# Fusing tokenizer and transformer on one core: the last weighted sum is handed over two images later, and the projection's loads get six buffers

## The chip, the cores and the metric

The kernel runs on one core of a Trainium2 chip, alone. The metric is device time in microseconds for one launch, and the number compared is the median of several executions. One execution is also recorded by the hardware profiler; that one has its own time and its own span (first to last instruction on the core).

Engine names in what follows: PE is the matrix engine (TensorE), DVE is VectorE, ACT is ScalarE, POOL is GpSimd, SP is SyncE. The first four compute; in the part of the kernel that matters here SP issues the large loads, and POOL issues the gathers, the scatters and the output.

## The reference, cut to what matters

A tokenizer of four Fourier layers (truncated 2-D FFT, per-mode mixing, pointwise mixing, batch norm) turns 64 images of 256 x 256 into 256 rows of width 256 each. 77 text rows are added to each, which gives 333 tokens. Then one pre-norm transformer layer follows, in which half of the tokens go through the feed-forward net:

```python
h = tok(x)                                  # 64 x 256 x 256, last step out = v @ q_w + q_b
h = concatenate([h, txt], axis=1)           # 64 x 333 x 256
h = h + attn(layernorm(h))                  # one head of width 256
z = layernorm(h)
weights = z @ wr + br                       # one router weight for each token
_, idx = top_k(weights, 166); sel = idx[:, :165]
y = (gelu(z[sel] @ w1 + b1) @ w2 + b2) * weights[sel]
h = h + (zeros.at[sel].set(y) + z)
```

The last line is the one concerned: for each token, the feed-forward row if it was selected (a zero row if not) times its router weight, plus the normalised row z and the residual h.

## The kernel before

The tokenizer's layers take the first 9.6 ms and are written in an order fixed by hand. The change touches only what follows. There the code is written as plain functions, image by image, and a scheduler orders the instructions of each engine: it weighs up, with costs of its own, what could start when. So the place of a call in the source is a wish, and the order in which an engine meets its instructions is that of the built program. [...]

For one image b these functions are called:

- `image_rows` projects the last Fourier layer to 256 rows. Eight chunks `ch` of 1 MB each are loaded from HBM by SP (line 909) and reduced by 32 matmuls (line 911, four for each chunk) into the accumulator `hp`, which ACT copies out as `h` (line 916). Chunks come from the pool `inp`; before the change it has seven buffers. SP can issue a load only once the matmuls that read the old content of the buffer are done.
- `attention`: layer norm (lines 922 to 943, the square root by ACT in line 928), queries (1009, 1013), scores (1023), softmax (1028 to 1030), values (1037, 1040), transposed probabilities (1052), product (1061), the sum with `h` and a bias added by POOL (1057, 1064). The second layer norm gives `fz`, stored by POOL in a table in HBM (line 1069).
- `select` ranks the tokens: it computes the router weights (955 to 962) and then, for three groups of tokens, the rank and a 0/1 matrix `place` (970 to 982), all on DVE.
- `fetch` turns `place` into row numbers `who` with small matmuls (994, two sets of three, and 997) and gathers the 165 selected rows as `zr` by two indirect DMAs from POOL (998).
- `feed_forward` transposes `zr` (1079, copied out as `zs`), multiplies by w1 (1087, eight blocks; ACT copies each out as `g` with the gelu, line 1091), multiplies by w2 (1098, 1102), transposes back (1108), stores the rows `ys` in a second table in HBM (POOL, 1111), gathers them back to token order as `o` by three indirect DMAs from POOL (1115; tokens that were not selected fetch a zero row), and adds `z` to the residual on POOL (1118).
- `finish` is the last weighted sum: three instructions on DVE (line 1124), `o * fw + h1`, then 17 stores to the output from POOL (1129, 1133).

All POOL transfers carry one of eight semaphores in turn, and a transfer waits until the one eight before it has landed. PSUM accumulators named `pp` come from a pool of six, so a block of line 1087 can start when the accumulator six places before it has been copied out.

The loop at the end of the program is a software pipeline. In turn b it calls the rows of image b+2, the attention of b+1 (with the fetch of b inside it), the finish of b-1, the feed-forward of b, and the selection of b+1.

Of the kernel before, what the change touches and what calls it, by code (L numbers as in the profile page):

```python
# [9 lines left out]
F32 = mybir.dt.float32  # L10
# [128 lines left out]
def tile_fno_fusion_transformer(ctx: ExitStack, tc: tile.TileContext, a, cst_d, grid_d, out):  # L139
    nc = tc.nc  # L140
    x = a["x"].rearrange("b x y o -> b x (y o)")
    B = x.shape[0]
# [7 lines left out]
    def tables(pool, first, last, name):  # L150

        lo, hi = _AT[first][0], _AT[last][0] + _AT[last][1]
        t = pool.tile([128, hi - lo], F32, name=name)
        nc.sync.dma_start(t, cst_d[:, lo:hi])
        return lambda k: t[:, _AT[k][0] - lo:_AT[k][0] - lo + _AT[k][1]]
# [623 lines left out]
    src = vd[L % 2]  # L779
    s_, t_ = st  # L780
    tcon = ctx.enter_context(tc.tile_pool(name="tcon", bufs=1))
    inp = ctx.enter_context(tc.tile_pool(name="inp", bufs=7))
    tabt = tables(tcon, "exT", "tri", "cstt")
    EXT, MASK4, IOTA = tabt("exT"), tabt("mask4"), tabt("iota")
    TOKN = tabt("tokn").rearrange("p (t n) -> p t n", t=3)
# [15 lines left out]
    D = S  # L801
# [69 lines left out]
    tp = ctx.enter_context(tc.tile_pool(name="tt", bufs=2))  # L871
# [5 lines left out]
    def psum():  # L877
        return pp.tile([128, 512], F32, name="pp")
# [124 lines left out]
    def attention(b, h, between=None):  # L1003
        z, zT = layer_norm(h, "a")
        qT = tp.tile([128, 2, TOK], F32, name="qT")
        for eh in range(2):
            ps = psum()
            for dh in range(2):
                nc.tensor.matmul(
                    ps[:, :TOK], lhsT=wqk[:, dh, 128 * eh:128 * eh + 128], rhs=zT[:, dh, :],  # L1010
                    start=dh == 0, stop=dh == 1,
                )
            nc.scalar.activation(qT[:, eh, :], ps[:, :TOK], AF.Identity, bias=bqk[:, eh:eh + 1], scale=1.0)
        if between:
            between()
        v = tp.tile([128, 3, D + 2], F32, name="v")
        p_ = tp.tile([128, 3, TOK], F32, name="prob")
        sm = small.tile([128, 3], F32, name="sm")
        for t in range(3):
            r = rows[t]  # L1020
            ps = psum()
            for eh in range(2):
                nc.tensor.matmul(  # L1023
                    ps[:r, :TOK], lhsT=qT[:, eh, toks[t]], rhs=zT[:, eh, :], start=eh == 0, stop=eh == 1
                )
            scale = 1.0 / D ** 0.5
            mx = small.tile([128, 1], F32, name="mx")
            nc.vector.reduce_max(mx[:r], ps[:r, :TOK], axis=AX.X)
            nc.vector.tensor_scalar_mul(mx[:r], mx[:r], -scale)
            nc.scalar.activation(  # L1030
                p_[:r, t, :], ps[:r, :TOK], AF.Exp, bias=mx[:r], scale=scale, accum_out=sm[:r, t:t + 1]
            )
        for t in range(3):
            r = rows[t]
            ps = psum()
            for dh in range(2):
                nc.tensor.matmul(  # L1037
                    ps[:r, :D + 2], lhsT=zT[:, dh, toks[t]], rhs=wvE[:, dh, :], start=dh == 0, stop=dh == 1
                )
            nc.vector.tensor_add(v[:r, t, :], ps[:r, :D + 2], bvE[:r])  # L1040
            nc.vector.reciprocal(sm[:r, t:t + 1], sm[:r, t:t + 1])

            for n in range(2):
                nz = small.tile([128, 1], F32, name="nz")
                nc.vector.tensor_scalar(nz[:r], v[:r, t, D + n:D + n + 1], 0.0, None, ALU.not_equal)
                nc.vector.tensor_mul(sm[:r, t:t + 1], sm[:r, t:t + 1], nz[:r])
        pT = tp.tile([128, 3, TOK], F32, name="probT")
        for jt in range(3):
            r = rows[jt]
            ps = psum()  # L1050
            for t in range(3):
                nc.tensor.transpose(ps[:r, toks[t]], p_[:rows[t], t, toks[jt]], ID[:rows[t], :rows[t]])
            evict(pT[:r, jt, :], ps[:r, :TOK], 2)
        h1 = tp.tile([128, 3, D], F32, name="h1", bufs=3)
        for t in range(3):
            r = rows[t]
            nc.gpsimd.tensor_add(h[:r, t, :], h[:r, t, :], boB[:r])  # L1057
            ps = psum()
            for jt in range(3):
                rj = rows[jt]  # L1060
                nc.tensor.matmul(  # L1061
                    ps[:r, :D], lhsT=pT[:rj, jt, toks[t]], rhs=v[:rj, jt, 0:D], start=jt == 0, stop=jt == 2
                )
            nc.vector.scalar_tensor_tensor(
                h1[:r, t, :], ps[:r, :D], sm[:r, t:t + 1], h[:r, t, :], ALU.mult, ALU.add
            )
        z = layer_norm(h1, "f")
        for t in range(3):
            nc.gpsimd.dma_start(z_d[b % 3][128 * t:128 * t + rows[t]], z[:rows[t], t, :])  # L1069
        return h1, z  # L1070

    def feed_forward(b, h1, z, fw, idx, place, zr):

        zs = tp.tile([128, 2, KEPT], F32, name="zs")
        ps = psum()
        for c, k in enumerate(kept):
            n = k.stop - k.start
            for dh in range(2):
                nc.tensor.transpose(
                    ps[:, KEPT * dh + k.start:KEPT * dh + k.stop], zr[:n, c, 128 * dh:128 * dh + 128], ID[:n, :n]  # L1080
                )
        evict(zs.rearrange("p h k -> p (h k)"), ps[:, :2 * KEPT], 2)
        g = tp.tile([128, HID // 128, KEPT], F32, name="g", bufs=1)
        for hb in range(HID // 128):
            ps = psum()
            for dh in range(2):
                nc.tensor.matmul(  # L1087
                    ps[:, :KEPT], lhsT=w1[:, dh, 128 * hb:128 * hb + 128], rhs=zs[:, dh, :],
                    start=dh == 0, stop=dh == 1,
                )  # L1090
            nc.scalar.activation(
                g[:, hb, :], ps[:, :KEPT], AF.Gelu_apprx_tanh, bias=b1c[:, hb:hb + 1], scale=1.0
            )
        yT = tp.tile([128, 2, KEPT], F32, name="yT")
        for dh in range(2):
            ps = psum()
            for hb in range(HID // 128):
                nc.tensor.matmul(
                    ps[:, :KEPT], lhsT=w2[:, hb, 128 * dh:128 * dh + 128], rhs=g[:, hb, :],
                    start=hb == 0, stop=hb == HID // 128 - 1,  # L1100
                )
            nc.scalar.activation(yT[:, dh, :], ps[:, :KEPT], AF.Identity, bias=b2c[:, dh:dh + 1], scale=1.0)
        ys = tp.tile([128, 2, D], F32, name="ys")
        for c, k in enumerate(kept):
            n = k.stop - k.start
            ps = psum()
            for dh in range(2):
                nc.tensor.transpose(ps[:n, 128 * dh:128 * dh + 128], yT[:, dh, k], ID)
            evict(ys[:n, c, :], ps[:n, :D], 2)
        for c, k in enumerate(kept):  # L1110
            nc.gpsimd.dma_start(y_d[b % 3][k], ys[:k.stop - k.start, c, :])
        o = tp.tile([128, 3, D], F32, name="o")
        for t in range(3):
            r = rows[t]
            nc.gpsimd.indirect_dma_start(  # L1115
                o[:r, t, :], None, y_d[b % 3][:, :], bass.IndirectOffsetOnAxis(ap=idx[:r, t:t + 1], axis=0)
            )
            nc.gpsimd.tensor_add(h1[:r, t, :], h1[:r, t, :], z[:r, t, :])  # L1118
        return o, h1, fw

    def finish(b, o, h1, fw):
        for t in range(3):
            r = rows[t]
            nc.vector.scalar_tensor_tensor(  # L1124
                o[:r, t, :], o[:r, t, :], fw[:r, t:t + 1], h1[:r, t, :], ALU.mult, ALU.add
            )
        for g in range(4):
            for n in range(4):
                nc.gpsimd.dma_start(  # L1129
                    out[b, 64 * n + 16 * g:64 * n + 16 * g + 16].rearrange("(p t) d -> p t d", t=2),  # L1130
                    o[32 * g + 8 * n:32 * g + 8 * n + 8, 0:2, :],
                )
        nc.gpsimd.dma_start(out[b, S:TOK], o[0:TXT, 2, :])
# [1 line left out]
    hs = {n: image_rows(n) for n in range(min(2, B))}  # L1135
    done = attention(0, hs.pop(0))
    done += select(0, done[1])
    last = None
    for b in range(B):
        now, got = done, []  # L1140
        if b + 2 < B:
            hs[b + 2] = image_rows(b + 2)
        if b + 1 < B:
            done = attention(b + 1, hs.pop(b + 1), lambda: got.append(fetch(b, now[-1])))
        else:
            got.append(fetch(b, now[-1]))
        if last:
            finish(b - 1, *last)
        last = feed_forward(b, *now, *got)
        if b + 1 < B:  # L1150
            done += select(b + 1, done[1])
    finish(B - 1, *last)


# [31 lines left out]
```

## Time and profile before

| what | value |
|---|---|
| median of 3 runs | 12,647.37 us (12,644.53 to 12,658.94) |
| the profiled execution | 12,662.01 us, span 12,660.2 us |
| busy over the span | PE 88%, DVE 70%, ACT 48%, POOL 16% |
| from 9,811 to 12,541 us, the steady part of the loop | 2,730 us, PE busy 2,365.65 us, granted PE clock 0.90, DMA engines 64% |
| the fetches of line 998 in that part | one every 44.7 us on average |

The steady part is what the change touches: 64 images, of which all but the first and the last few follow one pattern of about 44.7 us. "Granted clock" is the share of full speed that the chip allows PE; the trace records it as intervals. The DMA share is the mean busy share of the core's 16 DMA engines in a stretch. In the waits view a line reads: who waited, at which line, for whom, then microseconds in total, number of times, longest.

### The profile page before, as it was taken

The numbers are of one execution on the slowest core, as the hardware profiler recorded it, in microseconds if no ns is written. First come the engines' busy times: TensorE is split into PE (matmuls) and PEld (weight loads), VectorE is DVE, ScalarE is ACT, GpSimd is POOL, SyncE is SP. The second block draws the span as 40 slices with busy tenths as digits, with TensorE's granted clock in tenths as the row PEclk, the third lists the DMA queues.
The fourth block names the chain that finished last, engine by engine and source line by source line (L and its number), as shares of the span: only waits on it lengthen the run. The fifth ranks groups of instructions, "written<-read, shape, count | busy, mean of one in ns | idle before, by whom it ended". The sixth has DMA issues, their size and how long they took to land. (4 is left out here: it accounts for less than half of the span.)

```text
span 12660.2 us, 404578 instructions
## 1 busy us (share of the span) xinstructions
PE 11148.0 (88%) x181142; PEld 5823.2 (46%) x181142; DVE 8876.0 (70%) x10892; ACT 6048.8 (48%) x10153; POOL 2037.2 (16%) x2630
## 2 busy tenths in 40 slices
PE   6999999997999999999979999999996888888887
PEld 3444444443444444444434444444443555555555
DVE  6777777777777777767667767677775666666665
ACT  5555555555555555545545545555553333333333
POOL 0000000001000000000010000000001455555555
PEclk7999999998999999999989999999997899889888
DMA  6555555556899998988888989889898666666664
GB/s 226 202 201 203 201 201 200 200 201 221 350 352 353 350 354 344 352 340 349 336 314 347 351 341 355 344 338 349 348 352 286 222 223 228 226 228 232 225 224 149
DMA packets 648775, 3550.85 MB, mean 280 GB/s; under 512 B 136632, under 2 KB 187320, under 8 KB 248056
## 3 DMA queue, kind: packets, MB, share of 16 engines
q1 hardware_dynamic: 539520, 3392.85, 69.8%
q0 software_dynamic: 100368, 128.39, 4.2%
q8 instruction: 1417, 23.22, 0.7%
q10 hardware_dynamic: 7144, 3.72, 0.1%
q14 instruction: 326, 2.67, 0.1%
HBM read 1794.51 MB, written 1729.56 MB: 278 GB/s over the span
## 5 line engine op out<-in xcount | busy, mean ns | idle before, releaser
L669 ACT ACTIVATE ring<-ring 128x1024 f32<-128x1024 f32 x3072 | 3108.8, 1012 | 1192.8 <-PE ring L662 1154.5
L650 DVE STREAM_TRANSPOSE t<-vo 128x2048 f32<-128x2048 f32 x1536 | 3549.9, 2311 | 174.9 <-ACT vo L645 14.4
L662 PE MATMUL ring<-vo,w 32*32 32x512 f32 x49152 | 2852.8, 622 | 391.2 <-DVE zt L689 138.9
L645 ACT ACTIVATE vo<-ring 128x1024 f32<-128x1024 f32 x1536 | 1568.2, 1021 | 3006.2 <-PE ring L638 2392.4
L646 DVE TENSOR_SCALAR vo<-ring 128x1024 f32<-128x1024 f32 x1536 | 1858.1, 1210 | 603.6 <-PE ring L638 415.0
L679 PE MATMUL ring<-t,cst 32*32 32x512 f32 x49152 | 1874.4, 605 | 311.4 <-issue 310.6
L689 DVE STREAM_TRANSPOSE zt<-ring 128x1024 f32<-128x1024 f32 x384 | 711.5, 1924 | 1678.5 <-PE ring L679 1678.5
L597 POOL TENSOR_TENSOR ams<-am,sk 48x512 f32<-48x512 f32 x384 | 486.9, 1268 | 8650.8 <-DMA am<-mix 8331.5
L662 PEld LDWEIGHTS ring<-vo,w 32*32 32x32 f32 x49152 | 763.6, 105 | 1905.2 <-ACT ring L669 478.6
L679 PEld LDWEIGHTS ring<-t,cst 32*32 32x32 f32 x49152 | 974.6, 104 | 1172.2 <-issue 726.6
L638 PE MATMUL ring<-vin,ws 32*32 32x512 f32 x32768 | 1239.5, 608 | 23.6 <-issue 21.6
L1129 POOL DMA_DIRECT2D out_dram<-o x1024 | 530.0, 530 | 808.4 <-DVE gt L979 394.2
L702 PEld LDWEIGHTS ring<-cst,zt 128*128 128x128 f32 x4608 | 535.4, 194 | 173.3 <-ACT vo L645 162.5
L669 ACT ACTIVATION_READ_ACCUMULATOR ring<-ring 128x1 f32 x3072 | 584.2, 190 | 0.0
L702 PE MATMUL ring<-cst,zt 128*128 128x96 f32 x4608 | 567.7, 280 | 6.7 <-DVE zt L689 6.7
L911 PE MATMUL hp<-ch,win 128*32 128x512 f32 x4096 | 469.0, 602 | 12.8 <-DMA ch<-v 12.7
L638 PEld LDWEIGHTS ring<-vin,ws 32*32 32x32 f32 x32768 | 253.4, 103 | 407.9 <-issue 375.7
L608 PE MATMUL ring<-ams,cst 49*128 49x512 f32 (+1 forms) x1536 | 391.5, 621 | 34.5 <-POOL ams L597 25.0
L1023 PE MATMUL pp<-azT,qT 128*128 128x333 f32 (+1 forms) x768 | 411.5, 690 | 0.0
L1124 DVE SCALAR_TENSOR_TENSOR o<-o,fw,h 128x256 f32<-128x256 f32 (+1 forms) x192 | 92.7, 483 | 397.7 <-DMA o<-yr,idx 262.4
L994 PE MATMUL pp<-cstt,place 128*83 128x2 f32 (+3 forms) x768 | 110.3, 248 | 282.4 <-DVE place L982 264.2
L1087 PE MATMUL pp<-zs,w 128*128 128x165 f32 x2048 | 319.6, 316 | 41.2 <-DVE zs L181 24.5
(940 smaller groups left out, 12260.0 us busy)
## 6 DMA issues: line engine op xcount, KB each, us to landing
v<-vo SPq DMA_DIRECT2D x1536, 1024.0 KB
vin<-v SPq DMA_DIRECT2D x1024, 1024.0 KB
ch<-v SPq DMA_DIRECT2D x512, 1024.0 KB
mix<-ob SPq DMA_DIRECT2D x96, 512.0 KB
am<-mix SPq DMA_DIRECT2D x384, 96.0 KB
xin<-in_x_dram SPq DMA_DIRECT2D x16, 1024.0 KB
mv<-in_x_dram SPq DMA_DIRECT2D x256, 64.0 KB
zr<-fz POOLq DMA_DIRECT2D x128, 128.0 KB, 2.0
```

The costliest lines, as they stand in the source:

```text
L597: nc.gpsimd.tensor_tensor(ams[b % 2][hv], a_[hv], sk[hv].rearrange("p c k -> p (c k)"), ALU.mult)
L638: nc.tensor.matmul(ps[n][32 * j:32 * j + 32], lhsT=ws[32 * n:32 * n + 32], rhs=v[32 * n:32 * n + 32, 2 * j:2 * j + 2, :], start=False, sto ...
L645: nc.scalar.activation(of[:, 0:2], t2[0], AF.Relu)
L646: nc.vector.tensor_scalar(of[:, 2:4], t2[1], 0.0, None, ALU.max)
L650: nc.vector.transpose(t32[b, t // 2][:, :, 8 * (t % 2):8 * (t % 2) + 8, :].rearrange("p y s c -> p s y c"), o.rearrange("p s (y l) -> p s ...
L662: nc.tensor.matmul(ps[n][32 * j:32 * j + 32], lhsT=w4[i + 1][32 * n:32 * n + 32], rhs=o[32 * n:32 * n + 32, 2 * j:2 * j + 2, :], start=Tru ...
L669: nc.scalar.activation(t2[n], t2[n], AF.Square, accum_out=acc[:, at:at + 1])
L679: nc.tensor.matmul(ps[n][32 * j:32 * j + 32], lhsT=FYT[32 * n:32 * n + 32, k, :], rhs=t32[b, j][32 * n:32 * n + 32, k].rearrange("p s c -> ...
L689: nc.vector.transpose(zt[:, h].rearrange("p k c -> p c k"), t2[h].rearrange("p n (s c) -> p c (n s)", c=C),)
L702: nc.tensor.matmul(ps[:, 0, 96 * g:96 * g + 96], lhsT=zt[:, h, k0:k0 + 4, :].rearrange("p k c -> p (k c)"), rhs=FX[:, h, 48 * r:48 * r + 9 ...
L911: nc.tensor.matmul(hp[32 * g:32 * g + 32], lhsT=win[:, 7 - t:39 - t], rhs=ch[:, g], start=False, stop=t == 7, skip_group_check=True,)
L1129: nc.gpsimd.dma_start(out[b, 64 * n + 16 * g:64 * n + 16 * g + 16].rearrange("(p t) d -> p t d", t=2), o[32 * g + 8 * n:32 * g + 8 * n + 8 ...
```

## The change

Three edits. `finish` is called for image b-2 instead of b-1, with a list that holds two pending results; to keep the data alive, `h1` has four buffers instead of three and `o` three instead of two. And the pool `inp` for the projection's chunks has six buffers instead of seven.

```diff
@@ -779,7 +779,7 @@
-    inp = ctx.enter_context(tc.tile_pool(name="inp", bufs=7))
+    inp = ctx.enter_context(tc.tile_pool(name="inp", bufs=6))
@@ -1051,7 +1051,7 @@
-        h1 = tp.tile([128, 3, D], F32, name="h1", bufs=3)
+        h1 = tp.tile([128, 3, D], F32, name="h1", bufs=4)
@@ -1109,7 +1109,7 @@
-        o = tp.tile([128, 3, D], F32, name="o")
+        o = tp.tile([128, 3, D], F32, name="o", bufs=3)
@@ -1135,7 +1135,7 @@
-    last = None
+    last = []
     for b in range(B):
         now, got = done, []
@@ -1144,12 +1144,13 @@
             done = attention(b + 1, hs.pop(b + 1), lambda: got.append(fetch(b, now[-1])))
         else:
             got.append(fetch(b, now[-1]))
-        if last:
-            finish(b - 1, *last)
-        last = feed_forward(b, *now, *got)
+        if len(last) > 1:
+            finish(b - 2, *last.pop(0))
+        last.append(feed_forward(b, *now, *got))
         if b + 1 < B:
             done += select(b + 1, done[1])
-    finish(B - 1, *last)
+    for b, q in zip(range(B - len(last), B), last):
+        finish(b, *q)
```

## The prediction

> **What bounds the kernel now.** I read the waits of a steady stretch first (10,500 to 12,400 us, 43 images), then stretches of 4 us through one image for the clock, then the instructions of single engines.
>
> ```profile
> POOL out_dram L1129 <- DVE gt L979: 303.3, 43, 8.1
> ...
> PE pp L994 <- DVE place L982: 183.0, 43, 6.8
> ...
> DVE o L1124 <- DMA o<-yr,idx: 179.1, 102, 5.4
> ...
> PEld hp L911 <- DMA ch<-v: 25.1, 30, 2.3
> ...
> PE pp L1079 <- DMA zr<-zr,who: 11.9, 15, 2.4
> ```
>
> PE waits 4.3 us in every image (183.0/43) at line 994 for the third `place`. On DVE that `place` stands behind the final sum, which waits for the gather of `o` (179.1/43 = 4.2 us). PE hardly waits for anything else: 0.3 us an image for `zr`. So gather of `o`, sum, `place`, PE is the chain.
>
> PE's own list of one image, from the first chunk matmul:
>
> ```profile
> 11156.19 7.07 PE L911 MATMUL hp<-ch,win 128*32 128x512 f32 x64
> 11163.20 2.51 PE L1009 MATMUL pp<-azT,wqk 128*128 128x333 f32 x8
> 11165.55 0.39 PE L994 MATMUL pp<-cstt,place 128*83 128x2 f32 x4
> 11171.06 0.44 PE L994 MATMUL pp<-cstt,place 77*83 77x2 f32 x2 [5.12 <-DVE place L982]
> ```
>
> And what the stall does to the clock (columns: stretch, its length, busy PE, weight load, DVE, ACT, POOL, granted clock, DMA share, GB/s):
>
> ```profile
> 11164.00:11168.00 4.00, 1.94 (x11) 1.26 (x9) 1.05 (x4) 1.91 (x3) 0.00 (x0) 1.00 0.96 281
> 11172.00:11176.00 4.00, 4.00 (x13) 2.56 (x12) 2.19 (x10) 2.00 (x3) 3.07 (x2) 0.50 1.02 412
> 11180.00:11184.00 4.00, 3.61 (x21) 2.76 (x20) 3.12 (x22) 2.82 (x9) 0.00 (x0) 1.00 0.80 260
> 11184.00:11188.00 4.00, 3.48 (x19) 2.64 (x17) 2.89 (x8) 0.52 (x1) 2.02 (x4) 1.00 0.11 27
> ```
>
> After the gap PE runs at half clock until 11,178.75 (the clock's intervals: 10.24 us at 0.5 from 11,168.5). So a gap of 5 us costs about 3.5 us more. The same lines show the DMA engines full until 11,184, with the chunk loads.
>
> There are two kinds of image in turn: in A, ACT copies out `zs`; in B, DVE does. ACT's list around line 1091 in an A:
>
> ```profile
> 11142.94 0.43 ACT L179 COPY zs<-pp 128x330 f32<-128x330 f32 x1 [4.41 <-PE pp L1079]
> 11143.40 1.28 ACT L928 ACT_TABLE_LOAD   x1
> 11144.69 0.30 ACT L928 ACTIVATE frs<-fmv,epsc 128x3 f32<-128x3 f32 x1
> 11145.00 1.28 ACT L1091 ACT_TABLE_LOAD   x1
> 11146.30 2.42 ACT L1091 ACTIVATE g<-pp,b1c 128x165 f32<-128x165 f32 x8
> ```
>
> PE meanwhile runs line 1087 from 11,143.43 for 4.76 us and goes straight on to line 1098 (11,148.03): ACT's two table loads cost PE nothing here.
>
> [...] half-clock intervals of 3.41, 6.83 or 10.24 us, after gaps of about 2 us or more. [...] Here `zr` lands 1.4 us (spread 0.5) after the last chunk packet of the burst, whereas the first gather's time from issue varies between 10.5 and 15.7 us: it is the burst that sets the landing. [...] The trace shows the 1.28 us alone; the next operation starts 0.02 us later, and I use that.
>
> **The change part by part.** The order on each engine can be read from the built program before it runs.
>
> *The final sum.* It doesn't move. In both programs DVE meets the sum of tile `o` of an image between line 974 and line 976 of the next selection, right after POOL has issued that same `o`'s gather; POOL's 17 stores follow that gather in both. The scheduler hoists the later call to the place of the earlier one. So the wait of 4.2 us stays, and with it PE's gap and half clock: 0 gained. The added buffers of `o` and `h1` take away waits that don't show: 0. Nor does the tail of the program change: POOL's list of the last four images is the same but for single swaps.
>
> *The gather of `zr`.* `who` now comes right after `place` (before, layer-norm statistics stood between), and the first gather goes ahead of the sixth store, so it's issued some 0.9 us earlier (11,172.62, with the previous store over at 11,171.76 and one store 0.53). I count 0: the burst sets the landing. If that cover is gone, at most 0.9 us in A, where PE waits for `zr`.
>
> *The sixth buffer.* PE's lists from line 911 to 1023:
>
> ```
> before, A  911x28 943 1009x2 911x4 1009x2 994x3 1023 994x3 1023x5
> after,  A  911x24 943 1009x4 911x4 994x3 1023 994x3 1023x2 911x4 1023x3
> before, B  911x32 1009x4 994x3 1023 994x3 1023x2 ...
> after,  B  911x24 1009 911x4 1009x3 994x3 1023 911x4 994x3 1023x5
> ```
>
> The seventh chunk comes later, but still ahead of the stall. Its load is issued when the first chunk is used, as the eighth's was before; that arrived in time for a use 6.2 us into the projection, but for waits of 0.8 us (25.1/30). The new use is at 5.6 us in B and later in A: up to 1.4 us more, all inside the stall. The eighth chunk goes behind the stall. That is 8 of the 64 matmuls, 7.07 x 8/64 = 0.88 us, taken from a place where PE would wait anyway and added to where it is late. [...] I take 0.88 (0 if something later hides it; 1.77 if it's all paid at half clock). In B PE reaches line 1079 1.3 us after `zr` has landed (30.74 against 29.43 us after the first chunk matmul): all 0.88 counts. In A PE waits there for `zr` on average 11.9/21 = 0.57 us: 0.31 counts. The second half of the gather comes later in B (`who` waits behind the displaced chunk), some 0.7 us, which B's 1.3 us hide. SP's list keeps its order, the loads are the same 8 MB, and DMA is 64% busy: 0.
>
> *ACT's list.* `h` now comes later, so the square root of its layer norm does too, and the table loads (!) stand elsewhere:
>
> ```
> before, A  qT h qT !ars !prob x3 probT zs !frs !g x8
> after,  A  qT qT !prob h prob x2 probT !ars zs !g !frs !g x7
> before, B  h qT !ars qT !prob x3 probT x2 !frs !g x8
> after,  B  qT qT h !prob x3 !ars probT x2 frs !g x8
> ```
>
> B has one load fewer; it stands where line 1037 covers it: 0. A has one more, and it splits `g`: between the first and the second come load, `frs`, load: 1.28 + 0.30 + 1.28 = 2.86 us. On the times shown: line 1087 starts at 43.43 and the first block's `g` load about 0.9 later, at 44.35 to 45.63; `g` until 46.05, then 2.86, second `g` done at 49.3. The eighth block of 1087 needs that accumulator (six in the pool) and would start at 43.43 + 7 x 0.595 = 47.6. PE waits 1.75 us, and behind it in PE's list the rest of the feed-forward net, the next image's transposes and its chunk matmuls. Bounds: 0, and the 2.86. Line 1098 afterwards uses a `g` each 0.29 us, as fast as ACT delivers: no more.
>
> *Moved layer-norm work on DVE* (three `az`, 1.6 us) now stands between the sums of line 1064. PE's accumulators for the fifth block are needed 2.6 us after the last of these sums was done before: 0, with 1 us left.
>
> *Sum.* The new patterns hold for 28 images A and 27 B: 28 x (0.31 + 1.75) + 27 x 0.88 = 57.7 + 23.8 = 81.5 us. The profiled execution, 12,662.0, becomes 12,743.5. It stands 14.6 above the median of the runs; so 12,729.
>
> **Rivals.**
>
> 1. *Hidden after all.* The accumulators come free in time and something else takes up the displaced chunk: 12,647. For it: PE has 0.3 to 0.5 us of small waits in the image. Against it: B's PE is late at line 1079 by its own list.
>
> 2. *The new stall halves the clock.* 1.75 us is just below the gaps of 2.0 us that did so in this trace, and 1.6 with 0.5 did. One interval of 3.41 us costs 1.7: 28 x 1.7 = 48 more, 12,777; with the upper bounds of both terms (28 x 3.74 + 27 x 1.77 = 152) up to 12,850.
>
> 3. *The sum does run on older data*, the faster side. If in truth the sum meets data that landed an image ago, PE loses its gap (4.3) and the half clock (3.5): 55 x 7.8 = 430 us, 12,220. It decides only if `zr` then lands within 22 us of the first chunk matmul, when PE would get to it (7.07 + 2.51 + 0.39, then 15.97 from 11,171.06 to line 1079 less half of the 7.69 at half clock); from 24 us on a new gap of 2 us brings the half clock back at line 1079. `zr` lands at 29 to 30 with the burst, so even then most is lost. The order of the lists speaks against it.
>
> **How the numbers follow.** The sum as worked out: 0.52, own range 12,690 to 12,770. Half clock as well: 0.20. Hidden: 0.18. Faster, rival 3 or a gain that I don't see: 0.10. Within 0.2%, 25 us, is about what a measurement of this kernel can't tell from no change. Slower by more: 0.70, the first two without a low end of 0.02; the same 0.20; faster 0.10. The range, 12,640 to 12,815, leaves out the faster case and the top of rival 2.
>
> **What would show it.** Line 1124 waits for `o` as before, about 4 us an image, and line 994 for `place` too. Four matmul rows of line 911 stand after line 994. ACT shows in every second image a `g`, two table loads and seven `g`; line 1087 there waits about 1.7 us for ACT. The step from fetch to fetch is 46 to 46.3 us instead of 44.7. I'm wrong if the wait at line 1124 is gone, if line 1087 doesn't wait, or if the granted clock in the steady part moves by more than 0.02 from 0.90.

## The result

The changed kernel takes 12,746.33 us (median of four runs, 12,723.01 to 12,756.72), the kernel before 12,652.57 us beside it. The ratio is 1.0072, with a 95% interval of 1.0054 to 1.0089: slower by 94 us. The profiled execution took 12,756.72 us, with a span of 12,754.9 us against 12,660.2. The first 9,617 us, ahead of the loop that the change touches, are as they were (PE busy 8,613.92 us there, 8,617.85 before).

The waits of the steady stretch of the changed kernel, from 10,500 to 12,400 us (who waited, at which line, for whom: us in total, times, longest). The stretch now holds 41 images instead of 43:

```profile
DVE o L1124 <- DMA o<-yr,idx: 265.7, 123, 5.2
...
PE pp L994 <- DVE place L982: 203.2, 41, 6.7
...
PE pp L1087 <- ACT g L1091: 33.8, 19, 1.8
...
PEld hp L911 <- DMA ch<-v: 24.9, 29, 2.8
...
PE pp L1079 <- DMA zr<-zr,who: 4.9, 7, 1.1
```

The chain from the gather of `o` over the sum of line 1124 to `place` is still there: PE waits 203.2/41 = 5.0 us an image for `place`. The wait for `zr` has shrunk because PE now comes later; `zr` itself lands when it did (its landing times are given further down). One line is new: line 1087 waits for ACT's `g`, 33.8/19 = 1.78 us, in every second image.

One line of the kernel before has to be set beside these. Its wait at line 1124 stands in two lines of the view, and the prediction read only the first:

```profile
DVE o L1124 <- issue: 94.8, 25, 5.5
```

Together they are (179.1 + 94.8)/43 = 6.4 us an image, against 265.7/41 = 6.5 after. The wait didn't grow; it is only credited differently.

PE's own list of one image A of the changed kernel (start, busy us, engine, line, operation, count, and in brackets the idle time before it; the trace shows each matmul of these lines as two, so x8 is one chunk):

```profile
11161.59 1.06 PE L911 MATMUL hp<-ch,win 128*32 128x512 f32 x8 [0.25 <-DMA ch<-v]
11162.59 0.46 PE L994 MATMUL pp<-cstt,place 128*83 128x2 f32 x4
11167.87 0.44 PE L994 MATMUL pp<-cstt,place 77*83 77x2 f32 x2 [4.83 <-DVE place L982]
...
11172.70 1.94 PE L911 MATMUL hp<-ch,win 128*32 128x512 f32 x8
...
11186.00 4.20 PE L1087 MATMUL pp<-zs,w 128*128 128x165 f32 x28 [0.53 <-ACT zs L179]
11191.98 0.83 PE L1087 MATMUL pp<-zs,w 128*128 128x165 f32 x4 [1.78 <-ACT g L1091]
```

The seventh chunk's eight matmuls stand ahead of the stall, the eighth's behind it, at half clock (1.94 us instead of 1.06; the trace records a clock of 0.5 from 11,166.15 to 11,176.39). The load that they wait for had landed at 11,166.68, 1.19 us before the end of the gap of 4.83 us, but they start only at 11,172.70, in their place in PE's list. Further down, the eighth block of line 1087 waits. ACT's list of the same image shows why:

```profile
11185.51 0.43 ACT L179 COPY zs<-pp 128x330 f32<-128x330 f32 x1 [2.83 <-PE pp L1079]
11186.91 1.28 ACT L1091 ACT_TABLE_LOAD   x1 [0.96 <-PE pp L1087]
11188.20 0.40 ACT L1091 ACTIVATE g<-pp,b1c 128x165 f32<-128x165 f32 x1
11188.62 1.28 ACT L928 ACT_TABLE_LOAD   x1
11189.91 0.30 ACT L928 ACTIVATE frs<-fmv,epsc 128x3 f32<-128x3 f32 x1
11190.23 1.28 ACT L1091 ACT_TABLE_LOAD   x1
11191.52 2.14 ACT L1091 ACTIVATE g<-pp,b1c 128x165 f32<-128x165 f32 x7
```

Load, one gelu, load, square root, load, seven gelus. PE's eighth block starts at 11,191.98, right after the second gelu.

The stall at line 1087 leaves the clock of this image alone: it is 1.00 in both stretches of 4 us (stretch, length, busy PE, weight load, DVE, ACT, POOL, granted clock, DMA share, GB/s):

```profile
11188.00:11192.00 4.00, 2.22 (x17) 1.97 (x15) 1.70 (x8) 3.93 (x7) 1.74 (x4) 1.00 0.00 0
11192.00:11196.00 4.00, 4.00 (x28) 4.00 (x29) 3.34 (x6) 2.06 (x7) 2.93 (x5) 1.00 0.26 85
```

Over 9,811 to 12,541 us the granted clock is 0.89, against 0.90 before.

Where the time went, taken from the start times of all images but the first six and the last nine, in the profiled execution of each kernel. T is the first chunk matmul of line 911, F the first matmul of line 1079 that follows it in the same turn of the loop. The kinds A and B of image are those of the prediction:

| us | before | after | difference |
|---|---|---|---|
| T to F, image B | 30.80 | 31.53 | +0.73 |
| T to F, image A | 30.46 | 30.97 | +0.51 |
| F of B to the next T | 13.91 | 14.02 | +0.11 |
| F of A to the next T | 14.14 | 15.85 | +1.71 |
| mean step from F to F | 44.65 | 46.15 | +1.50 |

All 63 steps together are 97.8 us longer.

### The profile page after: what moved, and what is told of

It is laid out like the page before. It is cut to its first block, busy times and chain, and to the rows that moved or that the text cites. A ratio compares the mean times of both kernels' runs of the same rounds, so it can differ in the third digit from the quotient of the medians.

```text
span 12754.9 us, 404420 instructions
## 1 busy us (share of the span) xinstructions
PE 11182.9 (88%) x181142; PEld 5786.1 (45%) x181142; DVE 8797.6 (69%) x10892; ACT 6060.9 (48%) x10151; POOL 2039.7 (16%) x2630
## 5 line engine op out<-in xcount | busy, mean ns | idle before, releaser
L669 ACT ACTIVATE ring<-ring 128x1024 f32<-128x1024 f32 x3072 | 3108.8, 1012 | 1188.5 <-PE ring L662 1151.9
L911 PE MATMUL hp<-ch,win 128*32 128x512 f32 x4096 | 536.7, 655 | 15.3 <-DMA ch<-v 14.9
```

What stands on the lines that cost most here:

```text
L669: nc.scalar.activation(t2[n], t2[n], AF.Square, accum_out=acc[:, at:at + 1])
L911: nc.tensor.matmul(hp[32 * g:32 * g + 32], lhsT=win[:, 7 - t:39 - t], rhs=ch[:, g], start=False, stop=t == 7, skip_group_check=True,)
```

## The experiments

Most of these kernels fix one place in an engine's list with an edge that sets the order of issue and makes nothing wait for an end:

```python
def behind(ins, first):          # ins is issued after first, on the same engine
    tc.add_manual_dep(ins.ins, first.ins.name, mybir.DependencyInfo(
        mybir.DependencyClass.NoSync, mybir.DependencyReason.DATA), reason="order")
```

The line numbers of these kernels are 8 to 20 higher than those of the kernel before; the text gives the original ones.

### The sixth buffer alone

```diff
-    inp = ctx.enter_context(tc.tile_pool(name="inp", bufs=7))
+    inp = ctx.enter_context(tc.tile_pool(name="inp", bufs=6))
```

> The kernel before with one edit: the pool of the chunk loads has six buffers; the call of the last sum stays one image later and no other buffer is added. Theory (all of the loss comes from the sixth buffer, through the order of instructions that it brings about): PE's and ACT's lists are those of the changed kernel, so the ratio to before is its 1.007, 12,735 to 12,755 us, with a fetch step of 46.2 us and a wait of 1.8 us for ACT at line 1087 in every second image. Rival (the later call costs too: in the changed kernel the wait for o on DVE grew from 4.2 to 6.5 us an image): 12,670 to 12,720. If the later call gains and hides a larger loss of the buffer: 12,780 or more.

Measured: 12,750.61 us, ratio 1.0083 (1.0070 to 1.0097). The step is 46.11 us, and the waits of the same stretch of this kernel show line 1087 waiting for ACT:

```profile
PE pp L1087 <- ACT g L1091: 35.6, 20, 1.8
```

PE's and ACT's lists in its trace are those of the changed kernel. So the buffer alone gives the whole loss, and the later call with its two extra buffers gives nothing that can be measured beside six buffers. The rival here leaned on a growth of the wait for `o`, which, as shown above, didn't happen. The opposite experiment, the later call with seven buffers, was not run.

### The changed kernel without the split gelus

```diff
-        nc.scalar.activation(rs, mv[:, :, 1], AF.Sqrt, ...)
+        mark[name] = nc.scalar.activation(rs, mv[:, :, 1], AF.Sqrt, ...)
...
-            nc.scalar.activation(g[:, hb, :], ..., AF.Gelu_apprx_tanh, ...)
+            gelu = nc.scalar.activation(g[:, hb, :], ..., AF.Gelu_apprx_tanh, ...)
+            behind(gelu, mark["f"])
```

> The changed kernel, with the gelus of line 1091 held behind the square root of the next image's second layer norm (line 928) in ACT's list; no other list changes. Theory: the table loads between the first and the second gelu are worth what PE waits there, 1.75 us in each of 28 images A: 49 us less than the changed kernel, 12,690 to 12,705 us; step ending in A falls from 45.0 to about 43.2, step ending in B stays 47.4 us. Rival (PE's 1.8 us at line 1087 would only move to the next wait, for place): 12,735 or more.

Measured: 12,709.24 us, ratio 1.0039 (1.0025 to 1.0053). The wait of line 1087 for ACT is gone from the waits of that stretch, and F of A to the next T falls from 15.85 to 14.27 us, while T to F stays (31.47 and 30.86). The expectation named the wrong step: A's stall comes after A's own F, so it is the step that ends in B that falls (47.4 to 45.7 us). The gain is (1.0072 - 1.0039) x 12,655 = 42 us, a little under the 49 expected and, by the intervals of the two ratios, uncertain by some 28 us; the 63 steps of the two traces differ by 49.5 us. The stall was real time and didn't move on to the next wait.

### The changed kernel with all chunk matmuls ahead of line 994 again

```diff
-                nc.tensor.matmul(hp[32 * g:32 * g + 32], ...)
+                mark["rows"] = nc.tensor.matmul(hp[32 * g:32 * g + 32], ...)
...
-                nc.tensor.matmul(ps[:n, 2 * c:2 * c + 2], lhsT=place[:r, t, k], ...)
+                m = nc.tensor.matmul(ps[:n, 2 * c:2 * c + 2], lhsT=place[:r, t, k], ...)
+                behind(m, mark["rows"])
```

> The changed kernel, with the small matmuls of line 994 held behind the last chunk matmul of line 911, which gives PE the order it had before, with six buffers and the later call kept; ACT's list goes back to that of before by itself. Theory (order costs, not the number of buffers): 12,650 to 12,665 us, step 44.7 to 45.0; the eighth load is issued 0.9 us later than before, which may add a wait of up to 0.3 us at line 911. Rival (with six buffers the chunks are late): line 911 waits over 1 us an image and the time stays at 12,700 or more.

Measured: 12,647.83 us, ratio 0.9991 (0.9983 to 0.9999). With six buffers and the later call the kernel is back at the time of before, so the loss is one of order. The lists are not quite the old ones, though: on PE the seventh and the eighth chunk stand among or behind the queries of line 1009, and ACT, against what I expected, doesn't go back to its old list but has one table load fewer than before in A and in B, and none between the gelus. The waits of the same stretch, 43 images, say more (lines 919 and 1002 are the old 911 and 994):

```profile
PE hp L919 <- DMA ch<-v: 108.4, 47, 5.2
...
PE pp L1002 <- DVE place L990: 65.8, 23, 5.4
```

The chunks are late with six buffers, 2.5 us an image; I had expected up to 0.3. But the wait for `place` falls from 4.3 to 1.5 us, by about as much. My reading, which these totals fit and no run took apart: while PE waits for a chunk, `place` is on its way, and the wait that PE meets first takes its share from the other. The rival was right on the lateness, and it still costs nothing.

### The sum really later

What the later call asks for, but doesn't get, can be forced in the kernel before:

```diff
-            nc.vector.scalar_tensor_tensor(h1[:r, t, :], ps[:r, :D], ...)
+            mark["sum"] = nc.vector.scalar_tensor_tensor(h1[:r, t, :], ps[:r, :D], ...)
...
-            nc.vector.scalar_tensor_tensor(o[:r, t, :], o[:r, t, :], ...)
+            m = nc.vector.scalar_tensor_tensor(o[:r, t, :], o[:r, t, :], ...)
+            behind(m, mark["sum"])
```

> The kernel before (seven buffers, call one image later), with the last sum of line 1124 held behind the last sum of line 1064 of the next image in DVE's list: what the later call in the change asks for, but does not get. PE's list stays that of before. Theory: DVE no longer waits for o ahead of place, and PE's gap at line 994 with its half clock goes; but PE then reaches line 1079 at about 23 us after the first chunk matmul, and zr lands with the end of the chunk loads, at 27 to 29; the gap of 4 to 6 us and the half clock come back at line 1079: 12,560 to 12,760 us. Rival 3 of the prediction (the gap and the half clock are gained in full): 12,200 to 12,300.

Measured: 12,801.81 us, ratio 1.0116 (1.0100 to 1.0131), slower than my range. One image of PE's list in this kernel, in the columns used above (lines 1069, 1087 and 1095 are the old 1061, 1079 and 1087):

```profile
11132.66 0.54 PE L1002 MATMUL pp<-cstt,place 128*83 128x2 f32 x6
...
11141.00 4.25 PE L1069 MATMUL pp<-v,probT 128*128 128x256 f32 x18 [0.39 <-ACT probT L179]
11149.04 0.51 PE L1087 MATMUL pp<-cst,zr 83*128 83x83 f32 x2 [3.78 <-DMA zr<-zr,who]
11152.40 0.53 PE L1087 MATMUL pp<-cst,zr 82*128 82x82 f32 x2 [2.85 <-DMA zr<-zr,who]
11153.53 6.64 PE L1095 MATMUL pp<-zs,w 128*128 128x165 f32 x32 [0.59 <-DVE zs L181]
```

The gap at `place` is gone and a larger one stands at `zr`: 232.8 us in some 40 images of the stretch, 5.8 us each. The clock is halved behind it, as the stretch from 11,148 us shows (granted clock third from the end, 0.50):

```profile
11148.00:11152.00 4.00, 0.51 (x2) 0.29 (x2) 0.00 (x0) 0.00 (x0) 0.88 (x2) 0.50 0.87 262
```

T to F falls by 3.8 us in B and 0.2 in A, but F to the next T grows from 14.0 to 18.4, since the second half of `zr` is waited for there and the half clock now falls on the feed-forward net. Two smaller waits of PE grew as well: for the chunks (48.7 us in the stretch, 9.8 before), and for ACT at line 1087 (9.6 us in 12 images), since here too two table loads split the gelus. So moving the sum in earnest, with all else left as it was, loses more than the change did. Rival 3's amount (430 us) wasn't refuted, but its condition, that `zr` lands within 22 us, isn't met here.

### A pause in the loads

If the burst of loads holds `zr` up, a pause in it should let `zr` land. The late sum is kept; the projection is taken apart, with n chunks where they were and 8 - n behind line 1061, ahead of line 1079; and the fetch is called after the scores, so that PE has work while `place` is made:

```diff
-        for t in range(8):
-            ch = inp.tile([128, 4, 2, S], F32, name="ch")
+        def chunks(these):
+          for t in these:
+            ch = inp.tile([128, 4, 2, S], F32, name="ch")
...
-                nc.tensor.matmul(hp[32 * g:32 * g + 32], ...)
+                m = nc.tensor.matmul(hp[32 * g:32 * g + 32], ...)
+                if t >= n and b > 1:
+                    behind(m, mark["prod"])      # last matmul of line 1061
+                mark["rows"] = m
+        def rest():
+            chunks(range(n, 8))
+            ...                                  # h as before
+        chunks(range(n))
+        return rest
...
         if b + 2 < B:
-            hs[b + 2] = image_rows(b + 2)
+            rest = image_rows(b + 2)
...                                              # attention(b + 1, ...)
+        if b + 2 < B:
+            hs[b + 2] = rest()
```

The transposes of `zr` (line 1079) are held behind `mark["rows"]`, and the matmuls of line 994 behind the last one of line 1023.

> The kernel before with the sum held late as in late_sum, and the projection of an image taken apart: six of its eight chunks where they were, the last two held behind the last matmul of line 1061 and ahead of line 1079; the fetch is called after the scores of line 1023. So two of the eight loads can only be issued some 20 us after the first chunk matmul, and the burst ahead of the gather of zr is 6 MB. Theory (zr lands with the end of the burst, and that is what late_sum waited for): at some 310 GB/s the burst ends at about 20 us and zr lands at 21 to 22, where PE gets to line 1079 at about 23: gap and half clock are gained for good, 55 x 7.8 = 430 us less than before, 12,200 to 12,350. Rival (the gather is slow whatever the burst): a wait of over 2 us at line 1079 with half clock, 12,550 or more.

> As split_6_2, with five chunks ahead and three behind: the burst is 5 MB and ends 3 us earlier, but PE is at line 994 0.9 us earlier, so that place (some 10.5 us after the first chunk matmul when DVE doesn't wait) may come up to 1 us too late for it. Theory: zr lands at 18 to 19 us, no wait at line 1079; within 40 us of split_6_2, better if that one still waits for zr, worse if the wait for place grows. Rival (the gather is slow whatever the burst): no better than split_6_2.

> As split_6_2, with four chunks ahead and four behind: the burst ends at about 14 us. PE is at line 994 about 8.6 us after the first chunk matmul, some 2 us ahead of place. Theory: zr is early, but a gap of 1.5 to 2.5 us at line 994 or behind it comes back and brings the half clock in a part of the images: 12,300 to 12,500, slower than split_5_3.

> The projection taken apart four and four, with the sum left where it is before, between line 974 and line 976. Theory (the sum's wait for o sets place, and place sets PE): place comes at about 15 us as before, PE gets to line 994 3.5 us earlier and waits that much longer; the four late chunks then stand behind the stall: 12,600 to 12,850, no gain from the split by itself. Rival (the length of the burst alone sets the pace; with the shorter burst o lands earlier and so does the sum): 12,300 to 12,500.

| n ahead, behind | us | ratio to before | wait for `zr`, us an image | mean step |
|---|---|---|---|---|
| 6, 2 | 12,630.85 | 0.9988 (0.9979 to 0.9997) | 6.1 | 44.76 |
| 5, 3 | 12,317.45 | 0.9736 (0.9704 to 0.9768) | 1.5 | 39.42 |
| 4, 4 | 12,228.41 | 0.9664 (0.9648 to 0.9680) | 0.0 | 37.23 |
| 4, 4, sum and fetch left in place | 12,821.47 | 1.0135 (1.0115 to 1.0156) | 0.0 | 47.62 |

The first line of PE's waits from 10,500 to 12,000 us, with six and two (1098 is the old 1079):

```profile
PE pp L1098 <- DMA zr<-zr,who: 204.0, 49, 7.3
```

The same line with four and four (1012 is the old 994):

```profile
PE pp L1012 <- DVE place L1000: 23.2, 15, 2.4
```

And with the split alone:

```profile
PE pp L1012 <- DVE place L1000: 228.5, 32, 9.2
```

PE waits for `zr` with six and two (and less with five and three), for `place` with the split alone, and with four and four for neither by much. I had the sequence upside down: six and two should have been the best of the three, and was worth almost nothing; four and four came out faster than its range. I had taken 310 GB/s for the loads from the start, which is about their average in the kernel before (8.59 MB by 27.5 us after T in images B, by 28.8 in A). The rate of the chunk loads in GB/s, from the DMA packets of 40 images, in slots of 2 us after T, and for six and two also by kind of image:

```
from, us      2    4    6    8   10   12   14   16   18   20   22   24   26   28
six, two    165  209  224  277  257  347  409  409  384  258  316  311  327  188
four, four  207  394  411  413  302  241  114   16    1  184  326  343  333  308
six, two: A   6   19   62  340  325  364  415  409  399  367  347  231  339  346
six, two: B 323  399  385  215  189  330  403  408  368  150  284  391  316   30
```

The average of six and two hides two cases. In images B the first chunk load is issued 1.1 us after T. The six loads have moved their 6.3 MB by 22 us, which is about the 310 GB/s that I had taken, and the burst thins out; still `zr` comes at 24.7 us instead of 21 to 22, and PE waits 3.2 us for it. In 19 of the 20 images A the first load is issued more than 5 us after T. The reason stands in SP's own list (T is at 10,728.11 in this image; lines 899 and 918 are the old 891 and 909):

```profile
10733.42 0.30 SPq L899 DMA_DIRECT2D am<-mix  x1
10733.81 3.17 SPq L918 DMA_DIRECT2D ch<-v  x6
```

The small load of `am`, an input of `image_rows`, stands ahead of the chunks, and it waits until DVE has read the old content of its buffer (line 897); the chunks wait behind it, although their buffers come free from 1 us after T on. In these images 5.4 MB are moved by 22 us, the last two loads are issued at 22 to 23 us, the burst never pauses, and PE waits 9.5 us for `zr`. With five and three the same happens in 12 of 20 images A, with four and four in none: there the first load is issued at 1.8 us in A, the loads almost stop from 16 to 20 us, and `zr` is there when PE comes. So the pause is not all that sets six and two apart from four and four; the late load of `am` is the other part, and no run moved it by itself.

The split alone makes things worse, as expected: PE reaches `place` sooner and waits 7.1 us for it (228.5/32). Late sum alone +1.2%, split alone +1.4%, both with the later fetch -3.4%. Each takes away the cause of one of two waits that lie one behind the other; what the later fetch adds, the next section shows.

PE's list for one image B of the kernel with four and four, in the columns used above, has no gap over 0.2 us but the 0.77 us at `zs` (lines 1080, 920, 1098, 1107, 1118 are 1061, 911, 1079, 1087, 1098):

```profile
11036.83 4.16 PE L1080 MATMUL pp<-v,probT 128*128 128x256 f32 x18
11040.92 3.64 PE L920 MATMUL hp<-ch,win 128*32 128x512 f32 x32
11044.50 0.51 PE L1098 MATMUL pp<-cst,zr 83*128 83x83 f32 x4
11045.77 4.76 PE L1107 MATMUL pp<-zs,w 128*128 128x165 f32 x32 [0.77 <-DVE zs L181]
11050.37 2.69 PE L1118 MATMUL pp<-g,w 128*128 128x165 f32 x18
```

### What the gain needs, and six buffers again

```diff
 split_4_4_six:           pool "inp" with bufs=6 instead of 7
 split_3_5:               n = 3
 split_4_4_early_fetch:   fetch called ahead of the scores, its matmuls not held
```

> split_4_4 with six buffers in the pool of the chunk loads instead of seven; PE, ACT and POOL meet their work in the same order as there. Theory (the sixth buffer costs through order, and through lateness only where chunks are used in one piece): four buffers come free at once and the chunks behind them are needed 20 us later, so 12,200 to 12,270, the same as split_4_4 within 0.3%. Rival (six buffers make chunks late): line 911 waits over 1 us an image, 12,290 or more.

> As split_4_4, with three chunks ahead and five behind. In split_4_4 zr is no longer waited for (0.4 us in 40 images) and place is waited for 0.6 us an image at line 994. Theory (zr only needs a pause in the loads, and a shorter first piece brings nothing more): PE is at line 994 0.9 us earlier and waits that much longer for place, with the half clock in some images: 12,260 to 12,400. Rival (a shorter first burst still speeds up zr and with it PE): 12,220 or less.

> split_4_4 with the fetch called where it was before, ahead of the scores of line 1023; the sum is held late and the projection taken apart as there. Theory: the split and the late sum make the gain together and the place of the fetch a small part of it: PE waits for place 2 to 3.5 us more at line 994, with the half clock in most images, 12,350 to 12,560, still well under before. Rival (without the later fetch nothing is left of the gain): 12,620 or more.

Measured: 12,201.83 us with six buffers, ratio 0.9645 (0.9629 to 0.9661); 12,304.58 with three and five, 0.9726 (0.9710 to 0.9742); 12,464.94 with the early fetch, 0.9862 (0.9843 to 0.9881). All three fall as the theory said. The wait for `place`, from 10,500 to 12,000 us, orders them: 13.9 us in total with six buffers, 44.8 with three and five, 97.0 with the early fetch. So the late sum and the split by themselves are worth 1.4%, and the later fetch brings the rest of the 3.4%; the later fetch without the split was not run. The sixth buffer costs nothing where order is fixed, and this kernel is the fastest found, 3.55% under the kernel before, though its interval overlaps that of seven buffers (0.9648 to 0.9680). One stretch of the loop, 9,811 to 11,900 us, in the columns of the stretches above, for the kernel before:

```profile
9811.00:11900.00 2089.00, 1808.84 (x10489) 1233.75 (x10488) 1343.42 (x4697) 671.75 (x1372) 1054.45 (x1516) 0.90 0.64 226
```

The same stretch for four and four with six buffers:

```profile
9811.00:11900.00 2089.00, 2012.04 (x12726) 1384.21 (x12725) 1534.28 (x5689) 881.01 (x1727) 1319.76 (x1842) 1.00 0.75 272
```

PE is busy 96% of the stretch instead of 87%, at full clock, and does 21% more matmuls in it.

## Why the prediction was right, point by point

- *The sum doesn't move.* Right. In both traces DVE runs its three instructions between lines 974 and 980 of the next selection. Line 1124 waits 6.5 us an image for `o` as it did (6.4), and line 994 still waits for `place`. The later call by itself is worth nothing: six buffers alone give 1.0083, the whole change 1.0072. The step's figure for the wait, 4.2 us, was too low, since a second line of the view holds the rest; nothing in the sum used it.
- *The gather of `zr` earlier: 0.* Right. In A it lands 30.42 us after T (30.45 before), in B 29.56 (29.45).
- *The eighth chunk behind the stall.* Predicted +0.88 in B and +0.31 in A; T to F grew by 0.73 and 0.51. The sum of the two, 1.24, is close to the 1.19 of the prediction, but B's part was too high by 0.15 and A's too low by 0.20; that these cancel is luck, and no experiment took the difference apart. The 0.88 was an estimate, with as much half clock in an image as before; the half-clock intervals that the trace records from 9,811 to 12,541 us (3.41 to 13.65 us each) make it 8.9 us an image before (542.7 us in all) and 9.7 after (573.4).
- *ACT's two table loads between the gelus.* Predicted 1.75 us in each A; line 1087 waits 1.78, F of A to the next T grows by 1.71. Taking the loads away gave 42 us back.
- *The sum of terms.* Predicted 81.5 us, measured 94. The amount for a pair of images was right (2.94 predicted; +3.06 by the table, of which 0.11 in B after F was not foreseen). The term that was mis-sized is the number of images: I counted the 55 with the steady pattern, but all 63 steps are longer. The first six add 14.9 us, the 48 of the table 71.7, the last nine 11.3. At the two ends the table loads are the small part: without them 21 of the 26 us remain. What lengthens the ends so, no run took apart.
- *Rival 1, hidden.* Refuted: taking away the table loads gave 42 us back, and putting all chunk matmuls ahead of line 994, which takes both terms away, gave all of the loss back. The displaced chunk wasn't taken away by itself; its share is what is left without the table loads, 12,709 against 12,658, some 51 us where the sum had 32; 21 of them lie at the two ends.
- *Rival 2, half clock from the new stall.* Refuted: the clock stays at full speed (1.00) through the stall shown above, and of 25 such gaps that stand alone between 10,000 and 12,400 us one was followed by half clock.
- *Rival 3, the sum on older data.* Its reason for failing holds: with the sum forced late, PE waits 5.8 us for `zr` and the time is 12,802. Its amount comes out in another kernel: once `zr` lands ahead of PE and the fetch is called later, the kernel is 425 us faster with four and four, against the 430 worked out from the gap and the half clock. An image is shorter by 7.4 us; in the stretch from 9,811 to 11,900 us, where PE is busy 1,996.49 us and the clock is 0.99, that is 4.3 us less of idle time and 3.1 us less of busy time.

## What to carry to other kernels

A buffer count changes more than the time at which transfers start: it can change the order into which a scheduler puts other engines' work, so read each engine's list, not only the DMA times. That goes for SP too: with six and two, a small load that waited for its buffer held up the large ones behind it (first chunk load 5.7 us after T in the image A shown, 1.1 in images B). Before a wait is removed, ask which wait comes next and what ends it; here two waits lay one behind the other, taking away the cause of either alone lost 1.2 to 1.4%, taking away both gained 1.4%, and 3.4% with the fetch called later as well. The small gather behind the burst of large loads needed a pause in the burst here (PE's wait for `zr`: 5.8 us an image with the late sum alone, 0.0 with four and four), and the pause could be made by spreading the work that frees the buffers.

## What the runs showed of the hardware that was not expected

- Gap length alone didn't decide here whether PE's clock was halved. Of the gaps of 1.6 to 2.0 us that stand alone (no other above 1.2 us within 8 us before), those at line 1087 in the changed kernel and in the one with six buffers alone were followed by half clock in 1 of 49 cases, those at line 994 in the one with the early fetch in 14 of 18. Gaps of over 3 us that stand alone were followed by it in every case between 10,000 and 12,400 us, 44 of 44 in the kernel before and 48 of 48 in the changed one. So half clock came after a gap as short as 1.7 us (the one case at line 1087 in the changed kernel), and how often it did after such gaps differed between the two places; what makes the difference wasn't tested.
- A busy share of the DMA engines near 1 didn't mean one rate here. In the kernel before, over 40 images, all transfers together moved some 247 GB/s at a share of 0.95 from 8 to 10 us after T, and 420 GB/s at 1.01 from 14 to 16 us. In the slow slot POOL's small transfers take part with some 58 GB/s, in the fast one with 1.4; whether they are the cause wasn't tested.
